# A graph-attention layer on one core: carried rows copied by ScalarE out of PSUM, h fetched for finished blocks, and a new order on the SP queue

## The chip, the cores and the metric

The kernel runs on one core of a Trainium2 chip. The metric is the device time of a run in microseconds (us), the median of several runs. Beside the runs there is one execution taken by the hardware profiler; the "profile" or "trace" below is that one.

An engine of the core works through its own instruction stream in order: TensorE (PE), VectorE (DVE), ScalarE (ACT), GpSimd (POOL) and SyncE (SP). SP computes nothing here: it issues nearly all plain DMAs. GpSimd issues the gathers.

## The reference

200,000 edges (src, dst), sorted by dst, join 12,500 nodes with 256 features; 8 heads of 32. What is computed, cut to what matters:

```python
h = jnp.maximum(_layernorm(x, axis=-1), 0.0)
q, k, v = h @ Wq + bq, h @ Wk + bk, h @ Wv + bv          # each (n, HEADS, D)
logits = einsum('ehd,ehd->eh', q[dst], k[src]) / sqrt(D)
expv   = exp(logits - segment_max(logits, dst)[dst])
attn   = expv / segment_sum(expv, dst)[dst]
agg    = segment_sum(attn[:, :, None] * v[src], dst)
y      = h + gelu(agg + h @ Wskip + bskip)
out    = x + (layernorm(y) * gamma + beta)
```

## The kernel before

**Front.** `project` walks over the nodes in 98 blocks of 128. For each it computes h (norm and Relu), and k and v by two matmuls, and stores h in the table `h_tab`, k|v (512 columns) in `kv_tab`, and the two factors of the norm (reciprocal root, shifted mean) in `st_tab`. Beside it `make_plan` reads the edges and works out the tables that the main loop walks by.

**The main loop.** `walk_streams` cuts the edges into 8 streams (S) and 66 steps (NST). In a step every stream goes over 384 slots, 3 tiles (K) of 128 partitions. Slot 0 is no edge: it holds what the stream has summed up so far for the node at which the step begins, the *carried row* (8 denominators and 256 sums). In the loop of a step c:

- `gather`: 24 indirect DMAs by GpSimd, one per tile and stream, fetch 128 rows of `kv_tab` into a tile `kv`. The pool has 5 such tiles, and a step uses 3. Tiles 0 and 1 of step c+1 are asked for at the beginning of step c, tile 2 after the first `weigh`.
- `windows` (two to three steps ahead): eight DMAs fetch the h of the nodes that each stream meets in a step, 32 or 64 rows per stream; `turn_windows` and `queries` make q of them on PE.
- `hot_e`, `hot_n`: 0/1 matrices from slots to nodes and back, made from `near`, `near_n` and `et`.
- `spread` (q to the slots, PE), `times` (q times k, DVE, L1058), `total` (sum per head, DVE, L1067), `turn` (transpose, PE).
- `maxima`: two scans and a subtraction (L1087 to L1090, DVE), then exp (L1091, ACT); `turn_back` (PE, L1098).
- `weights`: ACT copies the 64 denominators of the carried rows out of the kv tile's first partition (`wden`, L1105) and then the weights (`vw`, L1107). `weigh`: weight times v (DVE, L1114), and for tile 0 the weights times `wden` (L1119). A tile's `weigh` is the last use of its kv buffer.
- `add_up(c, i)`: the weighted rows are summed per node on PE, in three groups i of streams (0 to 3; 4 and 5; 6 and 7). ACT copies the sums from PSUM to SBUF (`sums_w`, L1142). `carry` (below) sends the last row of each stream's sums to partition 0 of the next step's first kv tile by DMAs, into columns 248 to 511: for i = 0 four DMAs (L1157), for i = 2 two (L1161) that serve four streams. Then the sums go to `table` (L1147).

A step's loop in the code begins with `times(c, 2)` and ends with `times(c+1, 1)` and `add_up(c, 2)`.

**Finished blocks.** When all sums of a pair of 128-node blocks are in `table`, the pair is finished beside the loop by class `Pair`, over three steps: `fetch` (sums, x and the norm's factors, six DMAs, L802 to L804), `norm` (h from x, two activations, L808), `turn`, `divisors`, `skip`, `divide`, `add`, `gelu`, `stats`, `root`, then `factors`, `normal`, `shifted`, `scale`, `store` (two DMAs, L891). There are 46 such pairs, and the six last ones (class `Last`) come after the loop, in the space of kv tiles.

**Order.** `keep` ties each instruction to the one before it on the same engine, so that the order of the code is the order on PE, DVE, ACT and SP. SP's order in a step with a pair, in `before`: six fetches, eight windows, two stores, four carries, four table writes, `et` and `pen` for step c+3, two table writes, two carries, two table writes. DMAs of a queue take turns at eight semaphores, so that a DMA is issued only when the eighth before it has landed.

Of the kernel before, what the change touches and what calls it, by code (L numbers as in the profile page):

```python
# [38 lines left out]
P = 128  # L39
# [5 lines left out]
S = 8  # L45
# [18 lines left out]
def gnn_kernel(ctx: ExitStack, tc: tile.TileContext, x, src, dst, Wq, bq, Wk, bk, Wv, bv,  # L64
# [17 lines left out]
    st_tab = dram.tile([NP, 2], F32, name="st_tab")  # L82
# [68 lines left out]
    def project():  # L151
# [12 lines left out]
        with tc.tile_pool(name="proj_c", bufs=1) as cpool, \  # L164
# [25 lines left out]
            def prepare(g):  # L190
# [14 lines left out]
                nr = pool.tile([P, 6, 2], F32, name="nr", bufs=3)[:, :n, :]  # L205
# [11 lines left out]
                return h, nr  # L217

            ready = {0: prepare(0)}
            for g, (b0, n) in enumerate(zip(starts, sizes)):  # L220
# [17 lines left out]
                h, nr = ready.pop(g)  # L238
# [9 lines left out]
                for tab, t in ((h_tab, h), (kv_tab, kvo), (st_tab, nr)):  # L248
                    nc.sync.dma_start(tab[b0 * P:(b0 + n) * P, :]
                                      .rearrange("(p b) d -> p b d", p=P), t)  # L250
# [21 lines left out]
    def finish(pool, psum, n, xt, sums, weights, mr, b_s, bet, o):  # L272
# [9 lines left out]
        h = pool.tile([P, n, HID], F32, name="h")  # L282
        for b in range(n):
            nc.scalar.activation(h[:, b, :], xt[:, b, :], AF.Relu, scale=mr[:, b, 1:2],
                                 bias=mr[:, b, 0:1])
# [46 lines left out]
    with tc.If(fits > 0) as branch:  # L332
        table = dram.tile([S, NT, SUMS], F32, name="table")
        walk_streams(tc, N, HID, NST, KL, ident, idx, d0_row, slot_row, near, near_n, e_tab, pen_tab,
                     h_tab, kv_tab, st_tab, table, x, out, w_q, w_s, one_row, b_q3, b_s3, b_o3,
                     gam, eps)
    with branch.Else():
# [4 lines left out]
        with tc.tile_pool(name="gfin", bufs=2) as pool, \  # L342
# [6 lines left out]
            for b0 in range(0, NBLK, NB):  # L349
                xt = pool.tile([P, NB, HID], F32, name="x_f")  # L350
                sums = pool.tile([P, NB, SUMS], F32, name="sums")
                mr = pool.tile([P, NB, 2], F32, name="mr_f")
# [9 lines left out]
                for t, tab, w in ((sums, gtab, SUMS), (mr, st_tab, 2)):  # L362
                    nc.sync.dma_start(t, tab[b0 * P:(b0 + NB) * P, :w]
                                      .rearrange("(b p) d -> p b d", p=P))
                s4 = sums.rearrange("p b (h d) -> p b h d", h=HEADS)
                finish(pool, psum, NB, xt, s4[:, :, :, :D], s4[:, :, :, D], mr, b_s, bet, o)
# [313 lines left out]
def make_near(tc, near, near_n, late):  # L680

    nc = tc.nc
    wide = S * WN
    with tc.tile_pool(name="near", bufs=1) as pool:
# [14 lines left out]
        for out, cols in ((near, wide), (near_n, near_n.shape[1])):  # L701
# [11 lines left out]
            else:  # L713
                for s, at in NARROW.items():
                    iota(grp[:, at:at + WNN], [[0, WNN]], s)
                iota(n[:, :P], [[0, 4], [1, WNN]])
                iota(n[:, P:], [[0, 4], [1, WN]])
# [18 lines left out]
            if cols < wide:  # L736
                ends = pool.tile([6 * S, 1], F32, name="near_e")
                nc.vector.tensor_sub(ends, pick[:, 3:4], pick[:, 5:6])
                for a, w in ((0, WNN), (P, WN)):
                    last = slice(a + w - 1, a + 4 * w, w)  # L740
                    nc.vector.tensor_scalar(out[:, last], grp[:, last], ends, None, op0=OP.mult)


def walk_streams(tc, N, HID, NST, KL, ident, idx, d0_row, slot_row, near, near_n, e_tab, pen_tab, h_tab,
                 kv_tab, st_tab, table, x, out, w_q, w_s, one_row, b_q3, b_s3, b_o3, gam,
                 eps):
# [31 lines left out]
    class Pair:  # L778
# [7 lines left out]
        def places(self):  # L786
            self.sums = self.pool.tile([P, 2, SUMS], F32, name="sums")
            self.x = self.pool.tile([P, 2, HID], F32, name="x_f")
            self.mr = self.pool.tile([P, 2, 2], F32, name="mr_f")
            self.h = self.pool.tile([P, 2, HID], F32, name="h", bufs=1)  # L790
# [6 lines left out]
        def fetch(self):  # L797
# [3 lines left out]
            for b, (node, row) in enumerate(zip(nodes, rows)):  # L801
                self.keep(nc.sync.dma_start(self.sums[:, b, :], tab[ds(row, P), :]))  # L802
                self.keep(nc.sync.dma_start(self.x[:, b, :], x[ds(node, P), :]))
                self.keep(nc.sync.dma_start(self.mr[:, b, :], st_tab[ds(node, P), :]))  # L804

        def norm(self):
            for b in range(2):
                self.keep(nc.scalar.activation(self.h[:, b, :], self.x[:, b, :], AF.Relu,  # L808
                                               scale=self.mr[:, b, 1:2], bias=self.mr[:, b, 0:1]))
# [79 lines left out]
        def store(self):  # L889
            for b, node in enumerate(loaded(slot_row[0:1, self.m, 0:2], N - P)):  # L890
                self.keep(nc.sync.dma_start(out[ds(node, P), :], self.y[:, b, :]))  # L891

    class Last(Pair):
# [3 lines left out]
        def __init__(self, pool, m, room, small, ps_h, ps_o, keep):  # L897
            Pair.__init__(self, pool, m, ps_h, ps_o, keep)
            self.room, self.mr = room, small
# [10 lines left out]
        def fetch_rows(self):  # L910
            self.places()
            for b, node in enumerate(loaded(slot_row[0:1, self.m, 0:2], N - P)):
                self.keep(nc.sync.dma_start(self.x[:, b, :], x[ds(node, P), :]))
                self.keep(nc.sync.dma_start(self.mr[:, b, :], st_tab[ds(node, P), :]))
# [6 lines left out]
    with ExitStack() as es:  # L921
# [199 lines left out]
        def add_up(c, i, tiles=range(K)):  # L1121
# [21 lines left out]
            if c + 1 < NST and i != 1:  # L1143
                carry(c, i)
            for s in streams:
                _, at, w = where(s)
                keep(nc.sync.dma_start(table[s, ds(g["nodes"][s], w - 1), :],  # L1147
                                       g["sums"][at:at + w - 1, i, :]))

        def carry(c, i):  # L1150


            sums, kv = step[c]["sums"], step[c + 1]["kv"][0][0:1, :, HID - HEADS:]
            if i == 0:
                for s, at in NARROW.items():
                    r = at + WNN - 1
                    keep(nc.sync.dma_start(kv[:, s:s + 1, :], sums[r:r + 1, 0:1, :]))  # L1157
            else:
                for b in range(2):
                    r = b * WN + WN - 1  # L1160
                    keep(nc.sync.dma_start(kv[:, 4 + b::2, :], sums[r:r + 1, 1:3, :]))  # L1161
# [28 lines left out]
        for j in range(K - 1):  # L1190
# [4 lines left out]
            turn(0, j)  # L1195
        pair = before = None
        for c in range(NST - 1):

            pair_next = None
            if c in due:  # L1200
# [5 lines left out]
                pair_next.fetch()  # L1206
# [7 lines left out]
            if pair:  # L1214
                pair.norm()
# [9 lines left out]
            if before:  # L1225
                before.scale()
                before.store()
# [15 lines left out]
            if tiles_of(c + 1) == K:  # L1243
                gather(c + 1, K - 1)
            if pair:
# [46 lines left out]
        assert len(rest) <= 6  # L1292
        mrs = one.tile([P, 6, 2, 2], F32, name="mr_l")
        lasts, banks = [], {}

        def room(i):
            if i % 2 == 0:
                room.tile = gath.tile([P, S, KV], F32, name="kv").rearrange("p s d -> p (s d)")
            half = S * KV // 2
            return room.tile[:, i % 2 * half:i % 2 * half + half]  # L1300

        def bank(i):
            def get():
                if i % 2 == 0:
                    banks[i // 2] = qe_ps.tile([P, 2, 2, HID], F32, name="ps_qe")
                return banks[i // 2][:, i % 2]
            return get

        def last(i):
            if i < len(rest):  # L1310
                lasts.append(Last(fin, rest[i], room(i), mrs[:, i],
                                  lambda: hot_ps.tile([P, 2, KC, P], F32, name="ps_hot"),
                                  bank(i), keep))
                lasts[i].fetch_rows()

        for i in range(6):
            last(i)
# [3 lines left out]
        if pair:  # L1321
            pair.norm()
        for j in range(tiles_of(c)):
# [3 lines left out]
            if tiles_of(c) == K and j == 1:  # L1327
                total(c, K - 1)
        if tiles_of(c) == K:
            turn(c, K - 1)  # L1330
        if before:
            before.shifted()
            before.scale()
            before.store()
        for p in lasts[:2]:
            p.norm()
# [17 lines left out]
        for p in lasts[2:4]:  # L1354
            p.norm()
# [5 lines left out]
        for i in range(3):  # L1361
            add_up(c, i, range(tiles_of(c) - 1, tiles_of(c)))
        for p in lasts:
# [9 lines left out]
        for p in lasts[2:4]:  # L1373
            p.turn()
            p.skip()
        for p in lasts[4:]:
            p.norm()
        if pair:
            pair.store()
        for i, p in enumerate(lasts):  # L1380
            if i > 3:
                p.turn()
                p.skip()
# [5 lines left out]
        for i in range(len(lasts) + 2):  # L1389
# [7 lines left out]
            if i > 1:  # L1397
                lasts[i - 2].scale()
                lasts[i - 2].store()
# [344 lines left out]
```

## Time and profile before

| | |
|---|---|
| median of 3 runs | 3814.16 us (3803.91 to 3824.61) |
| the profiled execution | 2578.42 us, its span 2576.5 us |
| busy, PE / DVE / ACT / POOL | 1901.7 / 1931.5 / 957.7 / 1602.2 us |
| DMA | 588.25 MB, mean 228 GB/s |
| mean granted TensorE clock | 0.859 |

The runs take 1236 us longer than the profiled execution; nothing in the profile shows what for. "Busy" is the time in which an instruction is shown on the engine. A line such as "L1015 POOL DMA_INDIRECT kv<-kv_tab,idx x1576 | ..., ... | ..." gives line, engine, operation, what it writes and reads and how often, then busy time in us, mean ns of one, idle time of the engine just before such instructions, and what ended most of it. In the lines of the waits, "A <- B: t, n, m" says that A's engine stood still before A for t us in n places, at most m, until B was done. A wait for several things is put down to the last of them.

### The profile page before, as it was taken

Reading aid. Unit: us, or ns where it says so; the run is one execution under the profiler, and the core shown is the slowest. Engines: PE = TensorE matmul, PEld = TensorE weight load, DVE = VectorE, ACT = ScalarE, POOL = GpSimd, SP = SyncE. Lnnn points to the kernel's source line nnn. Section 1 sums busy time; section 2 is a strip of 40 time slices with the busy share of each in tenths; the row PEclk is TensorE's granted clock in tenths of the full one; section 3 lists DMA queues with packets and bytes.
Section 4 is the critical chain, followed back from the end, with each engine's and each line's share of the span. In section 5 each row is a group of like instructions: output and inputs, shape, how many; then the busy total and the mean of one; then the engine's idle time right before and its main releaser. Section 6 shows DMA issues by size and latency. Waiting matters only on the chain.

```text
span 2576.5 us, 35985 instructions
## 1 busy us (share of the span) xinstructions
PE 1901.7 (74%) x10240; PEld 1092.2 (42%) x10240; DVE 1931.5 (75%) x2228; ACT 957.7 (37%) x2111; POOL 1602.2 (62%) x1646
## 2 busy tenths in 40 slices
PE   6898776767777677777777777776777777767765
PEld 3443443434444444444444444444444444444433
DVE  7886677777777777777777787777777787777774
ACT  3432222222443443343443343443443443443433
POOL 2301776667766667677666777666767767667730
PEclk9999778777888988888898888888988988888887
DMA  7966887777877777777777777777777878777742
GB/s 257 321 233 206 242 241 224 220 215 232 241 233 230 233 233 230 231 235 237 232 226 229 235 238 236 232 235 235 235 229 238 241 231 234 232 227 234 238 139 64
DMA packets 283677, 588.25 MB, mean 228 GB/s; under 512 B 69931, under 2 KB 173852, under 8 KB 281288
## 3 DMA queue, kind: packets, MB, share of 16 engines
q0 software_dynamic: 128736, 423.23, 55.4%
q1 hardware_dynamic: 154202, 162.16, 19.8%
q8 instruction: 83, 1.36, 0.2%
q14 instruction: 126, 1.03, 0.1%
q10 hardware_dynamic: 530, 0.47, 0.1%
HBM read 500.90 MB, written 84.21 MB: 227 GB/s over the span
## 4 chain that ended last, share of the span: by engine, by line
POOL 26%; DMA 24%; DVE 22%; issue 15%; PE 8%; SPq 3%; ACT 2%; DVEq 0%; ACTq 0%; POOLq 0%
POOL kv L1015 26%; DMA kv<-kv_tab,idx 12%; DVE vw L1114 8%; DMA table<-sums_w 6%; DVE prod L1058 5%; PE ps_kv L244 4%; DVE L L1067 4%; DMA kv<-sums_w 3%; DVE st L855 1%; DMA x_in<-in_x_dram 1%; PE ps_qe L1048 1%; DVE sums L851 1%; SPq L1157 1%; DMA hw<-h_tab 1%; DMA e_tab<-row 1%
## 5 line engine op out<-in xcount | busy, mean ns | idle before, releaser
L1015 POOL DMA_INDIRECT kv<-kv_tab,idx x1576 | 1558.6, 989 | 677.1 <-issue 418.5
L1114 DVE TENSOR_TENSOR vw<-ps_x,kv 128x2048 f32<-128x2048 f32 x197 | 444.6, 2284 | 478.0 <-ACT vw L1107 402.1
L1048 PE MATMUL ps_qe<-qw,to_e 64*128 64x256 f32 x3152 | 468.6, 426 | 117.5 <-DVE prod L1058 117.0
L1058 DVE TENSOR_TENSOR prod<-ps_qe,kv 128x1024 f32<-128x1024 f32 x394 | 463.7, 1218 | 19.0 <-DMA kv<-kv_tab,idx 8.4
L1067 DVE TENSOR_REDUCE L<-prod 128x64 f32<-128x2048 f32 x197 | 450.3, 2286 | 6.7
L1048 PEld LDWEIGHTS ps_qe<-qw,to_e 64*128 64x128 f32 x3152 | 302.3, 203 | 276.8 <-DVE prod L1058 226.8
L1008 PE MATMUL ps_hot<-w_q,hwT 128*128 128x256 f32 x792 | 323.8, 570 | 1.3 <-ACT hwT L994 1.1
L1025 PE MATMUL ps_hot<-et,near 48*128 48x384 bf16 x264 | 105.5, 400 | 276.5 <-ACT qw L1010 251.0
L1008 PEld LDWEIGHTS ps_hot<-w_q,hwT 128*128 128x128 f32 x792 | 211.5, 284 | 103.2 <-issue 57.4
L1133 PE MATMUL ps_a<-vw,to_n 128*32 128x264 f32 (+1 forms) x2356 | 240.0, 439 | 3.9 <-DVE vw L1119 2.9
L244 PE MATMUL ps_kv<-w_kv,hT 128*128 128x512 f32 x392 | 186.8, 620 | 23.8 <-ACT hT L137 22.9
L1142 ACT COPY sums_w<-ps_a 128x264 f32<-128x264 f32 x131 | 49.7, 379 | 393.5 <-PE ps_a L1133 389.5
L955 ACT ACT_TABLE_LOAD x138 | 177.1, 1283 | 2.4
L1010 ACT COPY qw<-ps_hot 128x256 f32<-128x256 f32 (+1 forms) x132 | 62.3, 472 | 237.0 <-PE ps_hot L1008 237.0
L1133 PEld LDWEIGHTS ps_a<-vw,to_n 128*32 128x32 f32 (+1 forms) x2356 | 92.2, 126 | 133.7 <-issue 70.9
L1027 ACT ACTIVATE to_e<-ps_hot,ones 128x384 f32<-128x384 f32 x264 | 143.4, 580 | 9.5 <-PE ps_hot L1025 6.1
L1105 ACT COPY wden<-kv 1x64 f32<-1x64 f32 x66 | 16.0, 242 | 343.3 <-DMA kv<-kv_tab,idx 177.9
L1038 ACT ACTIVATE to_n<-ps_hot,ones 128x384 f32<-128x384 f32 x197 | 107.2, 579 | 90.3 <-PE ps_hot L1036 88.9
L244 PEld LDWEIGHTS ps_kv<-w_kv,hT 128*128 128x128 f32 x392 | 72.0, 194 | 107.3 <-issue 71.3
L1004 PEld LDWEIGHTS <-one_row 3*128 3x128 bf16 x132 | 12.6, 95 | 239.2 <-issue 236.9
L839 PE MATMUL ps_a<-w_s,hT 128*128 128x256 f32 x368 | 93.5, 398 | 22.3 <-ACT hT L825 22.3
L994 ACT COPY hwT<-ps_hot 128x256 f32<-128x256 f32 (+1 forms) x132 | 61.7, 468 | 127.0 <-PE ps_hot L991 122.4
(280 smaller groups left out, 2109.8 us busy)
## 6 DMA issues: line engine op xcount, KB each, us to landing
kv<-kv_tab,idx POOLq DMA_INDIRECT x1576
kv_tab<-kvo SPq DMA_DIRECT2D x14, 1536.0 KB
table<-sums_w SPq DMA_DIRECT2D x264, 65.0 KB
hw<-h_tab SPq DMA_DIRECT2D x264, 64.0 KB
pen<-pen_tab SPq DMA_DIRECT2D x66, 192.5 KB
sums<-table SPq DMA_DIRECT2D x92, 132.0 KB
x_f<-in_x_dram SPq DMA_DIRECT2D x92, 128.0 KB
out_dram<-o SPq DMA_DIRECT2D x92, 128.0 KB
```

The source lines that it names most:

```text
L244: ins = nc.tensor.matmul(ps_kv, hT[:, c, :], w_kv[:, c, :], start=c == 0, stop=c == KC - 1)
L955: keep(nc.scalar.activation(dummy[:, 1:2], dummy[:, 0:1], function))
L1008: keep(nc.tensor.matmul(ps[:, b, :], g["hwT"][:, b, k, :], w_q[:, k, :], start=False, stop=k == KC - 1, skip_group_check=True))
L1015: nc.gpsimd.indirect_dma_start(out=t[:, s, :], out_offset=None, in_=kv_tab[:, :], in_offset=bass.IndirectOffsetOnAxis(ap=idx[:, s, j, c:c ...
L1025: keep(nc.tensor.matmul(ps[:, :CH], near[:, i * P:(i + 1) * P], step[c]["et"], start=True, stop=True))
L1027: keep(nc.scalar.activation(step[c]["to_e"][:, i, :], ps[:, :CH], AF.Relu, scale=-1.0, bias=ones))
L1038: keep(nc.scalar.activation(step[c]["to_n"][:, j, :], ps, AF.Relu, scale=-1.0, bias=ones))
L1048: keep(nc.tensor.matmul(ps[:, b, a, :], g["to_e"][r, 2 * half + a, j * P:(j + 1) * P], g["qw"][r, (half + a) * half, :], start=True, stop= ...
L1058: keep(nc.vector.tensor_tensor(g["prod"][:, four, :].rearrange("p (a b) d -> p a b d", a=2), g["qe", half].rearrange("p b a d -> p a b d") ...
L1067: keep(nc.vector.tensor_reduce(g["L"][:, j, :].rearrange("p (s h) -> p s h", s=S), g["prod"].rearrange("p s (h d) -> p s h d", h=HEADS), A ...
L1114: keep(nc.vector.tensor_tensor(t[:, :, HEADS:].rearrange("p s (h d) -> p s h d", h=HEADS), wj[:, :, :, None].to_broadcast([P, S, HEADS, D] ...
L1133: keep(nc.tensor.matmul(ps[at:at + w, :], g["to_n"][:, j, i * P + at:i * P + at + w], g["vw"][j][:, s, :], start=j == 0, stop=j == tiles_o ...
```

## The change

- Row order: each stream's window begins with the carried row. `near_n` is made with its numbers one lower, so that the first column (it was the last) stands for the node that goes on, and the table gets rows 1 to w-1 in place of 0 to w-2.
- The carry: right after the copy of the sums, ACT copies one row per stream from PSUM to partition 0 of the next kv tile. The six DMAs of a step and the function `carry` go.
- h of a finished pair comes from `h_tab` by a DMA; `norm`, the table `st_tab` and the fetch of the factors go. h has two buffers in place of one.
- SP's order: `pair_next.fetch()` comes after `store(0)` and the last gather of the step, then `store(1)`; the store of a pair is cut into its two DMAs.
- The tail: rows of the last pairs are fetched in step NST-2; the third to sixth of them are turned and multiplied (`turn`, `skip`) ahead of their sums, the fifth and sixth in PSUM banks of `xt_ps` and `ag_ps`.
- The fallback path (not taken here) fetches h too.

```diff
             keep(nc.scalar.copy(g["sums"][:, i, :], ps))
-            if c + 1 < NST and i != 1:
-                carry(c, i)
+            if c + 1 < NST:
+                for s in streams:
+                    at = where(s)[1]
+                    keep(nc.scalar.copy(step[c + 1]["kv"][0][0:1, s, HID - HEADS:],
+                                        ps[at:at + 1, :]))
             for s in streams:
                 _, at, w = where(s)
                 keep(nc.sync.dma_start(table[s, ds(g["nodes"][s], w - 1), :],
-                                       g["sums"][at:at + w - 1, i, :]))
-        def carry(c, i):
-            sums, kv = step[c]["sums"], step[c + 1]["kv"][0][0:1, :, HID - HEADS:]
-            if i == 0:
-                for s, at in NARROW.items():
-                    r = at + WNN - 1
-                    keep(nc.sync.dma_start(kv[:, s:s + 1, :], sums[r:r + 1, 0:1, :]))
-            else:
-                for b in range(2):
-                    r = b * WN + WN - 1
-                    keep(nc.sync.dma_start(kv[:, 4 + b::2, :], sums[r:r + 1, 1:3, :]))
+                                       g["sums"][at + 1:at + w, i, :]))
...
-                self.keep(nc.sync.dma_start(self.mr[:, b, :], st_tab[ds(node, P), :]))
-
-        def norm(self):
-            for b in range(2):
-                self.keep(nc.scalar.activation(self.h[:, b, :], self.x[:, b, :], AF.Relu,
-                                               scale=self.mr[:, b, 1:2], bias=self.mr[:, b, 0:1]))
+                self.keep(nc.sync.dma_start(self.h[:, b, :], h_tab[ds(node, P), :]))
...
-                pair_next.fetch()
             if c + 3 < NST:
                 windows(c + 3)
...
-            if pair:
-                pair.norm()
...
                 before.scale()
-                before.store()
+                before.store(0)
...
             if tiles_of(c + 1) == K:
                 gather(c + 1, K - 1)
+            if pair_next:
+                pair_next.fetch()
+            if before:
+                before.store(1)
+            if c == NST - 2:
+                for i in range(6):
+                    last(i)
...
-        for p in lasts[2:4]:
+        for p in lasts[2:]:
             p.turn()
             p.skip()
-        for p in lasts[4:]:
-            p.norm()
         if pair:
-            pair.store()
-        for i, p in enumerate(lasts):
-            if i > 3:
-                p.turn()
-                p.skip()
+            pair.store(0)
+            pair.store(1)
+        for p in lasts:
             p.divisors()
             p.divide()
```

## The prediction

> **What bounds the kernel now.** I read the page first, then the line view of the scan at L1087 (one per step), the waits of VectorE, GpSimd and the SP queue, and last the timeline of a few steps. The scan starts give the length of a step:
>
> ```profile
> L1087 DVE TENSOR_TENSOR_SCAN ps_x<-pen,ps_x x66: 635/902/962, 284.9 to 2495.4; 64x384 f32<-64x384 f32 x65, 64x256 f32<-64x256 f32 x1
> ```
>
> (2495.4 - 284.9) / 65 = 34.01 us per step; the steps take 2210 of the span's 2576.5 us. Who fills a step? These are rows of the page, the same waits over the whole run, and the SP queue's waits:
>
> ```profile
> L1015 POOL DMA_INDIRECT kv<-kv_tab,idx x1576 | 1558.6, 989 | 677.1 <-issue 418.5
> ...
> L1105 ACT COPY wden<-kv 1x64 f32<-1x64 f32 x66 | 16.0, 242 | 343.3 <-DMA kv<-kv_tab,idx 177.9
> ```
>
> ```profile
> POOL kv L1015 <- issue: 418.5, 1373, 0.3
> DVE vw L1114 <- ACT vw L1107: 402.1, 57, 11.7
> ...
> POOL kv L1015 <- DVE vw L1119: 106.7, 37, 5.5
> ```
>
> ```profile
> DVE vw L1114 <- DMA hw<-h_tab: 75.9, 9, 9.7
> DVE o L887 <- PE ps_hot L881: 28.3, 45, 3.4
> ```
>
> ```profile
> SPq L1147 <- DMA table<-sums_w: 255.8, 128, 3.7
> SPq L802 <- DMA table<-sums_w: 162.8, 48, 5.2
> SPq L891 <- DMA out_dram<-o: 135.1, 47, 4.3
> ```
>
> GpSimd issues 24 gathers a step at 0.989 + 0.305 us (418.5/1373): 24 x 1.294 = 31.1 us of 34.0. VectorE stands still at one place only, the first weigh of a step (L1114): 402.1 + 75.9 = 478 us, 7.2 us in each of 66 steps. It waits for ScalarE's copies at L1107, which stand behind the copy of the carried row at L1105, and that one is idle 343 us. The timeline of one step shows for what (start, duration, instruction; in brackets the idle time before):
>
> ```profile
> 1221.53 0.38 ACT L1142 COPY sums_w<-ps_a 128x264 f32<-128x264 f32 x1 [3.04 <-PE ps_a L1133]
> ...
> 1228.73 1.84 SPq L1161 DMA_DIRECT2D kv<-sums_w  x2
> ...
> 1229.35 0.52 ACT L1091 ACTIVATE W<-W 64x384 f32<-64x384 f32 x1
> ...
> 1238.83 0.24 ACT L1105 COPY wden<-kv 1x64 f32<-1x64 f32 x1 [7.44 <-DMA kv<-sums_w]
> ...
> 1239.31 2.29 DVE L1114 TENSOR_TENSOR vw<-ps_x,kv 128x2048 f32<-128x2048 f32 x1 [10.42 <-ACT vw L1107]
> ```
>
> The row to be carried is in SBUF at 1221.91. Its DMA stands 7 us in SP's queue and needs another 8.3 us (1230.57 to 1238.83) until ScalarE goes on; VectorE loses 10.42 us. Where that DMA was in time, near the end of the run, the same wait is:
>
> ```profile
> 2469.10 2.29 DVE L1114 TENSOR_TENSOR vw<-ps_x,kv 128x2048 f32<-128x2048 f32 x1 [1.85 <-ACT vw L1107]
> ```
>
> The POOL row above closes the circle: the weigh frees the kv buffer for the next gathers, so GpSimd idles too (106.7 us booked on L1119, more on DMAs that released it later). So the carry sets the step, with GpSimd's own 31.1 us close beneath.
>
> [...]
>
> **The change part by part.**
>
> *Carry.* Six DMAs a step go (390 in all: x260 and x130). With them goes the wait at L1105 for a landing. What is late next: exp (0.52), in steps with a finished block the table load and its dummy (1.28 + 0.20), the wden copy (0.24) and two weight copies (0.30). That is the 1.85 us above; VectorE's part of such a step, from 1272.83 to the end of the divide at 1300.75, is 27.92 us without the wait. 27.92 + 1.85 = 29.8 us, below GpSimd's 31.1. Steps without a block are shorter on VectorE by the stats, factors, scale, divisors and divide (1.7 + 0.4 + 2.0 + 0.4 + 0.7 = 5.2 us) and fall on GpSimd more clearly.
>
> *Eight copies on ScalarE.* 1x264 from PSUM. The nearest rows: L1105 (1x64) 0.242, L1142 (128x264, same source and length) 0.379 us. I take 0.379: 3.0 us a step; the low end is 1.9. Behind the four of the first group stand the copy at L1078 and the next sums copy, behind the last two the normal() of the older block. In the step at 1250 the four would end about 1253.4, the root about 1254.7 against its need on VectorE at 1256.93; the last two would end at 1258.6, normal at 1259.7, needed at 1261.92. norm() leaves just this place (two activations, 1.09 us for the pair at 1221.81). So I charge nothing; if the cover were gone, 3.0 - 1.1 = 1.9 us a step, 124 us.
>
> *h fetched.* 46 pairs and 6 last ones, two blocks each, 128 KB in place of 1 KB: 104 x 128 KB = 13.6 MB on top of 588.25 (2.3%). Rows and h are asked for after store(0), in the step shown about 1264 to 1268, and turned in the next one at about 1295, 27 us later; the wait for the table writes (162.8 us on SP) falls away since those landed long before. Charge 0; the high end, if bytes set the time, comes as a rival.
>
> *SP's order.* 32 DMAs a step become 26; the fetch no longer stands ahead of the eight windows, and the second store no longer waits for the first with all the rest behind it. Nothing on SP feeds the recurrence of a step any more: windows are needed two steps later, table writes one step later (sums_w has one buffer, its next write is a step away). Charge 0.
>
> *Front.* st_tab's small stores go (14 of 6 KB and a few smaller), SP has slack there: 0 to -3 us; I take 0.
>
> *Tail.* The turn of the last full pair waited 6.17 us on PE for its hT, because ScalarE stood at norm() of rows just fetched; those norms and late rows go: -6. The turns of the fifth and sixth pair lie between 2536 and 2544, after the sums came; moved ahead, they lie beside the 8.7 us of sums DMAs: I take -5 (bounds 0 and -8). Together -11.
>
> *Sum.* A step goes to GpSimd's 31.1; I add 0.3 for coupling, since a gather may start only some 2.4 us after the weigh and VectorE at 29.8 leaves 1.3 us of room: 31.4. (34.01 - 31.4) x 65 = 170. With the tail -181: span 2576.5 to 2395.
>
> **From the profile to the time.** The profiled execution took 2578.42 us, the runs' median is 3814.16: 1236 us more, of which no view shows anything (the span leaves 1.9 us around it). Either it is a constant beside the kernel, and then 3814 - 181 = 3633; or it stretches all, 3814 x 2397/2578 = 3546; or the gathers are slower there, (3814 - 366) / 66 = 52 us a step, and then the carry's wait may lie in their shadow. Nothing in the profile decides; I take the constant, the plainest, and let the others widen the range.
>
> **The rivals.**
> 1. *Part of the stall comes back.* VectorE and GpSimd meet at one buffer, ScalarE's copies cost 1.9 us where I charged nothing: step 32.7, 85 + 11 = 96 less: 3718. For: no cover on ScalarE is over 3 us. Against: every such wait is absent in the step at 2469.
> 2. *The gap stretches with the kernel:* 3546.
> 3. *Nothing to gain in the runs:* gathers at 52 us a step hide the carry; only the tail shows: 3803. For: the unexplained 1236 us. Against: no engine is slow in the profile.
> 4. *Slower: bytes set the time.* Place: the DMA engines, queue q1 beside q0. The runs move 588.25 MB in 3814 us, 154 GB/s; 13.6 MB of h at that rate is 88 us, less 11 in the tail: 3891. It decides where the bytes of a step take longer than GpSimd's 31.1 us. For: busy share 0.79 in mid-run. Against: slice two of the page moved 321 GB/s, and a step at 31.4 us needs about 8.15 MB / 31.4 = 260.
> 5. *The carry still waits* (ScalarE's write to a row that a gather or VectorE still holds): the tile was gathered and its products taken before that copy, so I give it no number of its own; it falls under 1.
>
> **Chances.** Forecast 0.44, rival 1 0.17, rival 2 0.13, rival 3 0.08, rival 4 0.18. Within 0.5% (19 us, about what a measurement can tell from no change) lies rival 3 alone. Faster 0.74, same 0.08, slower 0.18. The range for 8 in 10 runs from 3510 (rival 2 with the 0.3 us of coupling gone: 19 us, and the tail's bound) to 3830, which leaves rival 4 out.
>
> **What would show it.** Right: L1157 and L1161 have no successor; VectorE's wait at the weigh is about 2 us; the scan's mean distance is 31 to 31.8 us; POOL's idle time besides issue falls from 259 (677.1 - 418.5) to under 100 us; ScalarE's busy time rises by some 197 - 52 = 145 us. Wrong: a new wait at L1058 for kv (gathers too late), POOL's issue gap growing beyond 0.305, landings that stretch, or a mean over 33. If the profile falls to about 2395 and the median does not move by as much, the step from profile to run was the wrong one.

## The result, and the profile after

| | before | changed |
|---|---|---|
| median of 4 runs | 3813.19 us (3803.91 to 3824.61) | 3776.2 us (3760.45 to 3781.26) |
| ratio | | 0.9895 [0.9853, 0.9936] |
| profiled execution | 2578.42 us, span 2576.5 | 3781.26 us, span 3779.5 |
| busy PE / DVE / ACT / POOL | 1901.7 / 1931.5 / 957.7 / 1602.2 us | 2353.9 / 1940.7 / 1080.3 / 1563.4 us |

Faster, by 1.05%, which is little but clear of the scatter (the runs of the two kernels do not overlap), and not by the 4.8% of the forecast. The two profiles cannot be set beside each other: that of the changed kernel is as long as its timed runs, that of before was 1236 us shorter than its own. So the profile after shows what the profile before did not, namely where the long runs spend their time. First the scan that marks the steps (view of one tile: duration min/median/max in ns, first and last start in us), then a row of the page and the waits:

```profile
L1078 DVE TENSOR_TENSOR_SCAN ps_x<-pen,ps_x x66: 635/902/962, 332.7 to 3705.4; 64x384 f32<-64x384 f32 x65, 64x256 f32<-64x256 f32 x1
```

```profile
L1006 POOL DMA_INDIRECT kv<-kv_tab,idx x1576 | 1523.1, 966 | 1893.8 <-DVE vw L1110 1397.4 <-issue 457.1 <-DMA kv<-kv_tab,idx 16.8
```

```profile
ACT sums_w L1133 <- remote: 1531.3, 96, 28.6
POOL kv L1006 <- DVE vw L1110: 1397.4, 63, 36.1
DVE rstd L855 <- ACT rstd L851: 759.0, 45, 21.8
...
PE ps_a L1124 <- issue: 410.1, 231, 6.2
...
DVE vw L1105 <- ACT vw L1098: 156.5, 66, 4.4
```

A step takes (3705.4 - 332.7) / 65 = 51.89 us. The last row is the wait that the change was about: 156.5 / 66 = 2.4 us a step, so the carry no longer holds VectorE up. The gathers are no slower than in the first profile (966 ns beside 989, and 457.1 / 1418 = 0.32 us of issue between them). What is new is the first row: ScalarE, which copies the sums of `add_up` out of PSUM, stands still 1531 us, 23 us a step, for something the view calls remote, that is, it found no instruction that ended just then. The semaphore that came last is TensorE's in all 96 of these waits; where a copy also waits for DMAs, these had landed at least 28 us before. GpSimd and VectorE stand behind it. The timeline shows one such wait (start, duration, instruction; idle time before in brackets):

```profile
1517.45 2.27 PE L1039 MATMUL ps_qe<-qw,to_e 64*128 64x256 f32 x16 [0.86 <-DVE prod L1049]
...
1519.65 0.66 PE L1124 MATMUL ps_a<-vw,to_n 128*32 128x264 f32 x8
...
1521.13 1.56 PE L1124 MATMUL ps_hot<-vw,to_n 128*64 128x264 f32 x12
...
1528.44 1.23 DVE L1049 TENSOR_TENSOR prod<-ps_qe,kv 128x1024 f32<-128x1024 f32 x1 [4.49 <-remote]
...
1534.03 0.28 PEld L1039 LDWEIGHTS ps_qe<-qw,to_e 64*128 64x128 f32 x1 [1.81 <-issue]
...
1537.55 0.38 ACT L1133 COPY sums_w<-ps_a 128x264 f32<-128x264 f32 x1 [19.87 <-remote]
```

The eight matmuls at 1519.65 are the last that the copy at 1537.55 needs, so their result is there only some 17 us after the trace shows them. This is the rule in such a trace: from the recorded end of these matmuls to the first copy of a step's sums it is 13.1 us here (median of 66 steps). I read this as matmuls that TensorE finishes well after their recorded end; that is my reading of these times, and no view shows what TensorE does in between. The windows of the same stretch (us; PE busy and count, PEld, DVE, ACT, POOL, granted clock, DMA share, GB/s):

```profile
1515.00:1520.00 5.00, 3.97 (x42) 1.95 (x40) 4.96 (x4) 2.66 (x5) 3.78 (x5) 1.00 0.72 206
1520.00:1525.00 5.00, 2.91 (x27) 1.48 (x20) 3.64 (x7) 0.00 (x0) 3.87 (x4) 1.00 0.61 190
1525.00:1530.00 5.00, 1.12 (x6) 0.55 (x7) 1.52 (x2) 0.00 (x0) 3.81 (x4) 0.86 0.71 202
1530.00:1535.00 5.00, 3.18 (x8) 1.46 (x8) 1.99 (x1) 0.00 (x0) 3.82 (x4) 0.50 0.72 208
1535.00:1540.00 5.00, 0.57 (x3) 0.29 (x3) 0.00 (x0) 1.75 (x5) 3.81 (x4) 0.50 0.70 203
```

42 matmuls appear in the first 5 us, then 27, 6, 8 and 3, while GpSimd goes on issuing gathers (3.8 of each 5 us). When the matmuls dry up at 1525 the recorded clock is still 1.00; it falls to 0.50 at 1528.6 (the record moves in steps of about 3.4 us). VectorE's product at 1528.44 waits for the second eight of the row at 1517.45, which ends at 1519.72: TensorE was nearly 9 us late before the record fell. From there to the copy at 1537.55 only the eight matmuls at 1519.65 are left in the order of the code, and they take 9 us where the record shows 0.66. So a clock halved at 1528.6 does not account for this wait. What the clock has to do with it in the whole run is counted further down.

### The profile page after: what moved, and what is told of

It reads as the page before. It is cut to its first block, busy times and chain, and to the rows that moved or that the text cites. A ratio compares the mean times of both kernels' runs of the same rounds, so it can differ in the third digit from the quotient of the medians.

```text
span 3779.5 us, 34981 instructions
## 1 busy us (share of the span) xinstructions
PE 2353.9 (62%) x10240; PEld 1275.8 (34%) x10240; DVE 1940.7 (51%) x2228; ACT 1080.3 (29%) x2527; POOL 1563.4 (41%) x1646
## 3 DMA queue, kind: packets, MB, share of 16 engines
q0 software_dynamic: 128736, 423.23, 38.3%
## 4 chain that ended last, share of the span: by engine, by line
another core or an unknown queue 42%; PE 31%; ACT 12%; DVE 7%; issue 6%; DMA 1%; DVEq 0%; ACTq 0%; SPq 0%; POOL 0%; POOLq 0%
PE ps_qe L1039 7%; PE ps_hot L999 5%; PE ps_kv L243 4%; ACT kv L1139 3%; PE ps_a L829 3%; DVE prod L1049 2%; PE ps_hot L871 2%; PE ps_a L1124 2%; ACT L946 2%; ACT to_e L1018 1%; ACT hwT L985 1%; DVE vw L1105 1%; PE ps_a L834 1%; PE ps_hot L982 1%
## 5 line engine op out<-in xcount | busy, mean ns | idle before, releaser
L1006 POOL DMA_INDIRECT kv<-kv_tab,idx x1576 | 1523.1, 966 | 1893.8 <-DVE vw L1110 1397.4
L1039 PE MATMUL ps_qe<-qw,to_e 64*128 64x256 f32 x3152 | 757.5, 540 | 562.1 <-issue 389.2
L1039 PEld LDWEIGHTS ps_qe<-qw,to_e 64*128 64x128 f32 x3152 | 458.0, 258 | 821.0 <-issue 555.1
L1124 PE MATMUL ps_a<-vw,to_n 128*32 128x264 f32 (+1 forms) x2356 | 396.0, 479 | 474.1 <-issue 410.1
L1105 DVE TENSOR_TENSOR vw<-ps_x,kv 128x2048 f32<-128x2048 f32 x197 | 444.7, 2285 | 156.5 <-ACT vw L1098 156.5
L1058 DVE TENSOR_REDUCE L<-prod 128x64 f32<-128x2048 f32 x197 | 450.4, 2286 | 6.7
L1124 PEld LDWEIGHTS ps_a<-vw,to_n 128*32 128x32 f32 (+1 forms) x2356 | 131.3, 140 | 738.3 <-issue 642.8
L999 PE MATMUL ps_hot<-w_q,hwT 128*128 128x256 f32 x792 | 249.3, 460 | 35.6 <-ACT hwT L985 35.3
L999 PEld LDWEIGHTS ps_hot<-w_q,hwT 128*128 128x128 f32 x792 | 164.8, 223 | 124.4 <-issue 60.5
L946 ACT ACT_TABLE_LOAD x138 | 177.1, 1283 | 2.4
L1124 PE MATMUL ps_hot<-vw,to_n 128*64 128x264 f32 x796 | 131.5, 400 | 49.2 <-issue 47.2
L1133 ACT COPY sums_w<-ps_hot 128x264 f32<-128x264 f32 x67 | 25.4, 379 | 435.0 <-remote 420.7
L1139 ACT COPY kv<-ps_a 1x264 f32<-1x264 f32 x390 | 143.9, 369 | 6.3
```

Of the source, the lines that this page charges most:

```text
L946: keep(nc.scalar.activation(dummy[:, 1:2], dummy[:, 0:1], function))
L999: keep(nc.tensor.matmul(ps[:, b, :], g["hwT"][:, b, k, :], w_q[:, k, :], start=False, stop=k == KC - 1, skip_group_check=True))
L1006: nc.gpsimd.indirect_dma_start(out=t[:, s, :], out_offset=None, in_=kv_tab[:, :], in_offset=bass.IndirectOffsetOnAxis(ap=idx[:, s, j, c:c ...
L1039: keep(nc.tensor.matmul(ps[:, b, a, :], g["to_e"][r, 2 * half + a, j * P:(j + 1) * P], g["qw"][r, (half + a) * half, :], start=True, stop= ...
L1058: keep(nc.vector.tensor_reduce(g["L"][:, j, :].rearrange("p (s h) -> p s h", s=S), g["prod"].rearrange("p s (h d) -> p s h d", h=HEADS), A ...
L1105: keep(nc.vector.tensor_tensor(t[:, :, HEADS:].rearrange("p s (h d) -> p s h d", h=HEADS), wj[:, :, :, None].to_broadcast([P, S, HEADS, D] ...
```

## The experiments

The runs came to five different chips, each time with the kernel before beside them. The chip (or the condition it was in; no chip was seen in both) turned out to matter more than any edit. In the column of before, 2588.41 and 2588.02 are medians of seven executions, and 2406.96 is one of four; the others in the table are single executions, as are all times below for which no range is given:

| chip | before | changed kernel | with plain transfers | gathers, fixed index |
|---|---|---|---|---|
| 4 | 2588.41 us | | 2228.76 | |
| 15 | 2588.02; 2596.47 | 2406.96 | | 2378.7 |
| 3 | 2576.1 | | | 2374.72 |
| 1 | 3822.28; 3830.12 | | 2242.48 | |
| 10 | 3816.9 | | | 3757.4 |

The median of the result belongs with chips 1 and 10 (before 3813), the profile before with chips 3, 4 and 15. Chips 4, 15 and 3 are called short below, 1 and 10 long. Letters of theories are explained where an expectation brings them in.

**On chip 4: the kernel before again, one part alone, one part undone, and the gathers replaced.**

`e0_before` is the kernel before without an edit:

> The kernel before, unchanged, to get a profile of a run that takes as long as the runs of the median. Theory A (the runs are held up by TensorE: while gathers land, its matmuls are finished many times later than their length, and everything that waits for them stands still): time 3.80 to 3.83 ms, a step of about 53 us, ScalarE's copies of the sums and VectorE's products wait for TensorE for over 10 us a step, and VectorE's wait at the first weigh (7.2 us a step in the 2578 us execution) is not what sets the step. Theory B (the same picture as in the 2578 us execution, only that each gather costs GpSimd more): 3.80 to 3.83 ms too, but a gather takes 2 us of GpSimd instead of 0.989 us and GpSimd has no idle time but issue. If the time is about 2580 us again, both are open and the chip differs from that of the runs.

2593.39 us, step (2509.5 - 284.0) / 65 = 34.24 us, and VectorE's wait for the carry as in the first profile:

```profile
DVE vw L1114 <- ACT vw L1107: 419.6, 57, 13.1
...
DVE vw L1114 <- DMA hw<-h_tab: 70.6, 9, 9.4
```

So the same kernel needs 2.59 ms here and 3.81 ms elsewhere; 1236 us that every run pays beside the kernel are ruled out.

`e1_carry_act` is the kernel before with the carry alone changed (and the row order that it needs); h is computed by `norm` as before, SP's order is the old one but for the six DMAs that go:

```diff
...
-            if c + 1 < NST and i != 1:
-                carry(c, i)
+            if c + 1 < NST:
+                for s in streams:
+                    at = where(s)[1]
+                    keep(nc.scalar.copy(step[c + 1]["kv"][0][0:1, s, HID - HEADS:],
+                                        ps[at:at + 1, :]))
...
```

> The kernel before with one part of the change: the carried row first in its window and copied by ScalarE out of PSUM; h is still computed, SP's order is the old one less the six carries. Theory A: the carry lies in the shadow of TensorE's wait, ratio to before 0.990 to 1.000, in any case not below 0.985. Theory C (the carry was on the path in the runs too, and the rest of the change lost what it won): ratio 0.95 or lower.

2396.69 us (2392.42 to 2406.74), ratio 0.9264 [0.9222, 0.9306]; step (2315.5 - 284.8) / 65 = 31.24 us.

```profile
POOL kv L1015 <- issue: 438.1, 1438, 0.3
...
DVE vw L1114 <- ACT vw L1107: 159.6, 66, 5.6
```

The carry alone brings all that the change brings on such a chip.

`e2_carry_dma` is the changed kernel with the carry sent by DMAs again:

```diff
-            if c + 1 < NST:
...
-                    keep(nc.scalar.copy(step[c + 1]["kv"][0][0:1, s, HID - HEADS:],
-                                        ps[at:at + 1, :]))
+            if c + 1 < NST and i != 1:
+                kv = step[c + 1]["kv"][0][0:1, :, HID - HEADS:]
+                if i == 0:
+                    for s, r in NARROW.items():
+                        keep(nc.sync.dma_start(kv[:, s:s + 1, :], g["sums"][r:r + 1, 0:1, :]))
...
```

> The changed kernel with the carry sent by DMAs again (from the first row of the window), all else as in the change: h fetched, SP's new order, the new tail. Theory A: ratio to before 0.990 to 1.000. Theory C: above 1.02, since then h and the new order cost what the carry wins.

2507.16 us (2505.22 to 2513.22), ratio 0.9688 [0.965, 0.9727]; step (2422.6 - 284.4) / 65 = 32.90 us.

```profile
DVE vw L1105 <- ACT vw L1098: 287.1, 47, 10.6
DVE vw L1105 <- DMA hw<-h_tab: 117.7, 19, 10.3
```

The rest of the change, without the new carry, shortens the step by 34.24 - 32.90 = 1.34 us. It touches the same wait from the other end: a carry goes out earlier. From the end of a step's last copy of sums to the end of the issue of its last carry it is 6.71 us in e0 and 5.34 here (mean of 65 steps), and the two rows of VectorE's wait add up to 490 us there and 405 here, 1.3 us a step less. That SP's new order does this, and not the fetch of h, is likely but was not tried by itself. The two gains overlap: once the row goes by ScalarE the rest is worth nothing (e1 on chip 4 against the changed kernel on chip 15, 31.24 and 31.43 us).

`e3_plain_pool` is the changed kernel with a plain transfer in place of each gather; the rows that the index names are left out, 256 KB of fixed contiguous rows are fetched:

```diff
-                nc.gpsimd.indirect_dma_start(
-                    out=t[:, s, :], out_offset=None, in_=kv_tab[:, :],
-                    in_offset=bass.IndirectOffsetOnAxis(ap=idx[:, s, j, c:c + 1], axis=0))
+                nc.gpsimd.dma_start(t[:, s, :], kv_tab[(s * 3 + j) * P:(s * 3 + j + 1) * P, :])
```

> The changed kernel with each indirect gather replaced by a plain DMA from GpSimd of the same 256 KB out of fixed, contiguous rows of the k|v table (the gather by index is left out, so the output is another one). Bytes, destinations, the queue and the buffers stay. Theory A1 (TensorE is held up by data landing in SBUF at some 200 GB/s): time stays within 5% of 3776 us. Theory A2 (it is held up by what is special in an indirect gather[...]): time falls below 2900 us.

2228.76 us; step (2152.7 - 278.6) / 65 = 28.83 us. With GpSimd relieved the next bound is 2.6 us below the 31.43 of the changed kernel (`e4_after`, next), near what the prediction gave VectorE (29.8 us in a step with a finished block, 5.2 less in one without). On this chip the run could not tell what holds TensorE up elsewhere, since it was not held up to begin with.

**On chip 15: the changed kernel itself, and h computed again.**

> The changed kernel, unchanged, beside the kernel before on one chip. Theory D (what differs between the 2578 us of the first profile and the 3776 us of the result is the chip or its condition, not the kernel): where the kernel before takes 2.58 to 2.60 ms, this one takes 2.36 to 2.41 ms, ratio 0.915 to 0.93, as the carry alone gave 0.926; where the kernel before takes 3.8 ms, this one takes 3.76 to 3.78 ms, ratio 0.985 to 0.995. Theory E (the changed kernel itself holds TensorE up while gathers land): 3.76 to 3.78 ms even where the kernel before takes 2.59 ms.

`e4_after`, the changed kernel without an edit: 2406.96 us (2402.7 to 2409.76), ratio 0.9298 [0.9257, 0.9338]. Its scan, GpSimd's row, its waits, and two windows of the stretch shown above (same columns):

```profile
L1078 DVE TENSOR_TENSOR_SCAN ps_x<-pen,ps_x x66: 634/902/962, 284.0 to 2326.7; 64x384 f32<-64x384 f32 x65, 64x256 f32<-64x256 f32 x1
```

```profile
L1006 POOL DMA_INDIRECT kv<-kv_tab,idx x1576 | 1546.2, 981 | 522.1 <-issue 434.3
```

```profile
POOL kv L1006 <- issue: 434.3, 1410, 4.8
ACT sums_w L1133 <- PE ps_a L1124: 345.7, 130, 11.0
...
DVE vw L1105 <- ACT vw L1098: 160.6, 66, 5.5
...
DVE prod L1049 <- DMA kv<-kv_tab,idx: 103.9, 41, 7.9
```

```profile
1520.00:1525.00 5.00, 3.96 (x35) 1.78 (x31) 4.91 (x8) 2.20 (x8) 3.78 (x5) 1.00 0.89 308
1525.00:1530.00 5.00, 3.98 (x29) 2.26 (x29) 4.89 (x6) 2.87 (x7) 3.78 (x5) 1.00 0.78 229
```

A step is (2326.7 - 284.0) / 65 = 31.43 us. Besides its own issuing GpSimd stands still 522.1 - 434.3 = 88 us, where it was 259 in the first profile: it waits for hardly anybody, which is how an engine looks that sets the time. ScalarE waits for the sums 345.7 us where it was 1531, and TensorE takes 35 and 29 matmuls per 5 us beside the same gathers. Theory D holds here, E falls.

`e5_no_hfetch` is the changed kernel with h computed from x and the factors again (`st_tab`, `norm` and the fetch of the factors put back):

```diff
-                self.keep(nc.sync.dma_start(self.h[:, b, :], h_tab[ds(node, P), :]))
+                self.keep(nc.sync.dma_start(self.mr[:, b, :], st_tab[ds(node, P), :]))
...
+        def norm(self):
+            for b in range(2):
+                self.keep(nc.scalar.activation(self.h[:, b, :], self.x[:, b, :], AF.Relu,
+                                               scale=self.mr[:, b, 1:2], bias=self.mr[:, b, 0:1]))
```

> The changed kernel with h of the finished blocks computed from x by two activations as before (factors of the norm fetched), all else as in the change: ScalarE's carry, SP's new order, the new tail. Difference to the changed kernel: 13.6 MB of DMAs against 104 activations. Theory D on a chip with 2.59 ms: within 0.7% of the changed kernel, since both are covered. If the h bytes cost time: at least 1% faster than the changed kernel. If ScalarE has no room for norm beside the carry's copies: 1% slower or more.

2407.95 us (2400.77 to 2412.59), ratio 0.9289 [0.9244, 0.9333]: no difference to the changed kernel. On such a chip the 13.6 MB cost nothing and save nothing.

> The kernel before once more, for its profile on the same chip as the two above. On a chip with 3.8 ms, theory A: TensorE finishes late while gathers land, ScalarE's copies of the sums wait for it over 10 us a step, gathers still take about 0.99 us of GpSimd each. On a chip with 2.59 ms: the profile of e0_before again, within 1%.

`e6_before_again`, the kernel before, on this chip: 2593.55 us, as on chip 4.

**On chip 1 (before 3822.28 us): before with a profile, and the plain transfers.**

> The kernel before, unchanged, for a profile on a chip of the kind on which it takes 3.8 ms, if this call comes to one. Theory D1 (there TensorE ends its matmuls late while gathers land, in the kernel before as in the changed one): the step of its loop is about 52 us, ScalarE waits some 20 to 29 us for add_up's matmuls in most steps, the gathers are still about 1 us of GpSimd each, and the wait of DVE vw for ACT vw is under 3 us a step, since it lies in the shadow of TensorE. Theory D2 (the kernel before is long there for another reason, its gathers or its small transfers): gathers well over 1.3 us each or the wait of DVE vw above 10 us a step. On a chip where it takes about 2590 us this says nothing new: span about 2590 and a step of 34 us.

`e7_before_slow`, the kernel before without an edit: 3830.12 us, and this is the execution that was profiled: a profile as long as the runs of the result.

```profile
L1087 DVE TENSOR_TENSOR_SCAN ps_x<-pen,ps_x x66: 635/902/962, 332.2 to 3747.7; 64x384 f32<-64x384 f32 x65, 64x256 f32<-64x256 f32 x1
```

```profile
ACT sums_w L1142 <- remote: 1564.3, 59, 30.3
DVE prod L1058 <- remote: 953.0, 88, 25.5
...
POOL kv L1015 <- DVE vw L1119: 799.4, 35, 34.6
...
DVE vw L1114 <- ACT vw L1107: 186.2, 61, 7.7
```

Step (3747.7 - 332.2) / 65 = 52.55 us, gathers 967 ns each, ScalarE 1564 us behind TensorE: theory D1. The first copy of a step's sums comes 25.9 us after the recorded end of its matmuls (median); in e0 and in e4 it is 0.07 us, at most 0.13. The wait that the change removes is here 186.2 us in all, 2.8 us a step, where it was 419.6 on chip 4. D2 falls.

> The changed kernel with a plain transfer of the same 256 KB in place of each gather by index (the rows that the index names are not fetched). On a chip where the kernel before takes 3.8 ms: theory A1 (any data landing in SBUF at this rate holds TensorE up): above 3300 us, with ScalarE still waiting over 15 us for add_up's matmuls. Theory A2 (only the gathers by index do[...]): under 2500 us. On a chip where before takes 2590 us: 2230 us, as the same kernel took before, which tells the two not apart.

`e8_plain_slow`, the kernel of `e3_plain_pool` on this chip: 2242.48 us, step (2167.9 - 286.3) / 65 = 28.95 us.

```profile
L1006 POOL DMA_DIRECT2D kv<-kv_tab x1576 | 854.9, 546 | 1041.2 <-DVE vw L1108 651.5
```

```profile
POOL kv L1006 <- DVE vw L1108: 651.5, 63, 13.1
ACT sums_w L1131 <- PE ps_a L1122: 330.8, 127, 10.9
```

On the chip where before takes 3822 us, the kernel with plain transfers is 14 us from its time on chip 4 (2228.76), and ScalarE waits 330.8 us for the sums in place of 1564, with the first copy again 0.07 us behind its matmuls. It lands the same bytes, at 267 GB/s over the span where the gathers there moved 153. So data landing does not hold TensorE up (A1 falls), the gathers by index do (A2). By what way these make TensorE late on the same chip (25.9 us in e7), no run shows.

**On chips 15, 3 and 10: the addresses or the instruction.** `e9_fixed_index`, `e11_fixed_index` and `e13_fixed_index` are one kernel: the gather instruction is kept, but all its indices are overwritten so that they name the same contiguous rows as the plain transfers (the rows of the plan are not fetched):

```diff
+        nc.gpsimd.iota(idx, pattern=[[K * P, S], [P, K], [0, NST]], base=0, channel_multiplier=1)
         walk_streams(tc, N, HID, NST, KL, ident, idx, d0_row, slot_row, near, near_n, e_tab, pen_tab,
```

`e10_half_plain` and `e12_half_plain` have plain transfers for the even streams alone:

```diff
             for s in range(S):
+                if s % 2 == 0:
+                    nc.gpsimd.dma_start(t[:, s, :], kv_tab[(s * 3 + j) * P:(s * 3 + j + 1) * P, :])
+                    continue
                 nc.gpsimd.indirect_dma_start(
```

> The changed kernel, still gathering by index, but every index names the same contiguous rows that the plain transfers read (the rows that the plan asks for are not fetched). GpSimd about 0.97 us a gather as before. On a chip where the kernel before takes 3.8 ms: theory A2a (the scattered addresses hold TensorE up) 2230 to 2450 us, ScalarE's wait for add_up under 5 us a step; theory A2b (the gather instruction itself does, wherever its rows lie) 3600 us or more, with that wait above 15 us a step. On a chip where before takes 2590 us it tells them not apart: about 2400, since GpSimd's issuing is what bounds it there.

> The changed kernel with every second gather (the even streams) made a plain transfer of the same size; the rows of those streams are not the ones that the plan asks for. On a chip where before takes 3.8 ms: if each gather by index holds TensorE up by its share, half of the 1370 us between the changed kernel and the one with plain transfers is left, about 2900 to 3000 us; if a few gathers at a time do no harm[...], 2300 to 2450; if any do the full harm, 3600 or more. On a chip where before takes 2590 us: between 2230 and 2407, near 2300, and nothing told.

Chip 15: 2378.7 and 2248.06 us.

```profile
L1007 POOL DMA_INDIRECT kv<-kv_tab,idx x1576 | 1526.9, 969 | 508.6 <-issue 435.6
```

Neither tells anything of the question, as the expectations say; the first shows that GpSimd's issuing, not the scatter of the rows, sets the 31 us step (969 ns a gather with contiguous rows).

> The kernel of e9_fixed_index again (gathers by index, all naming the same contiguous rows; the rows of the plan are not fetched). On a chip where before takes 3.8 ms: theory A2a (scattered addresses hold TensorE up) 2230 to 2450 us; theory A2b (the gather instruction does) 3600 us or more. On a chip where before takes 2590 us: 2379 us, as the same kernel took before, nothing told.

> The kernel of e10_half_plain again (every second gather a plain transfer of fixed rows). On a chip where before takes 3.8 ms: harm by the number of gathers, about 2900 to 3000 us; no harm from few at a time, 2240 to 2450; full harm from any, 3600 or more. On a chip where before takes 2590 us: 2248 us, as the same kernel took before, nothing told.

Chip 3: 2374.72 and 2234.05 us; the same again.

> The kernel of e9_fixed_index again (gathers by index, all naming the same contiguous rows; the rows of the plan are not fetched). On a chip where before takes 3.8 ms: theory A2a (scattered addresses hold TensorE up) 2230 to 2450 us; theory A2b (the gather instruction does) 3600 us or more. On a chip where before takes 2590 us: 2379 us, nothing told.

Chip 10, before 3816.9 us: 3757.4 us, step (3681.4 - 329.2) / 65 = 51.57 us.

```profile
ACT sums_w L1134 <- remote: 1531.6, 55, 28.9
POOL kv L1007 <- DVE vw L1111: 1402.1, 63, 32.9
```

With contiguous rows TensorE is held up as before (A2a falls, A2b stands): the first copy comes 25.6 us behind its matmuls. The plain transfers of e8 go over the same queue with as many packets and bytes (128736, 423.23 MB) from the same rows to the same places. So it is the gather instruction, wherever its rows lie; what of it, GpSimd's longer work for each (947 ns here, 546 in e8) or something else in it, is not separated. How the harm goes with the number of gathers was not seen, because no run of the half-plain kernel came to such a chip.

The last question is what the clock has to do with it. Counted from the traces: matmuls recorded as starting, per us of the stretches in which GpSimd issues its gathers or transfers without a gap of 0.6 us or more (from 400 us on to 200 us before the end); in all, then apart by the granted clock on record at the time, which is either 1.00 or 0.50; and the share of these stretches at 0.50:

```
                                all   clock 1.00   clock 0.50   share at 0.50
before, chip 4                 4.57      5.01         3.18           24%
before, chip 1                 2.32      4.36         1.01           61%
changed, chip 15               4.65      5.18         2.74           22%
changed, chip of the result    2.70      4.83         1.08           57%
plain transfers, chip 1        5.72      6.07         3.17           12%
fixed index, chip 10           2.51      4.60         0.91           57%
```

On a long chip matmuls start at about half the rate while gathers are issued, and most of the loss lies where the record says 0.50. Such times are longer there, and they are emptier: about one matmul per us, where a short chip at the same 0.50 starts about three. The three long traces have 66 stretches at 0.50 of 20 us or more each, about one a step; no other trace has more than eight. So half a clock by itself is not the explanation, but the clock is no bystander either. Which of the two brings the other about, the late matmuls or the 0.50, no run separates.

A step of the long kind then adds what otherwise overlaps. Its 24 gathers take 24 x (0.966 + 0.32) = 31 us, in which TensorE starts half its matmuls. GpSimd then waits 1397.4 / 66 = 21 us until TensorE, and VectorE behind it, have caught up and freed the buffers. 31 + 21 = 52 us, against 51.9 measured.

## Why the prediction was right and wrong

- **The step, 34.01 to 31.4 us: right, on the kind of chip where the profile before was taken.** Measured 34.24 (e0) to 31.43 (e4), and VectorE's wait at the weigh is 160.6 / 66 = 2.4 us (named: about 2). GpSimd is the bound by the signs that were named: idle time besides issue 522.1 - 434.3 = 88 us (named: under 100), and a step of 28.83 us once its instruction is cheaper (e3).
- **Eight copies at nothing: right.** 369 ns each against the 379 taken; ScalarE's busy time rose from 957.7 to 1076.9 us, 119 and not 145, and e1 with the copies in place has the shortest step of the chip-4 kernels that gather all rows.
- **h at nothing: right** (e5). **SP's order at nothing: right beside the new carry;** that without it the rest of the change saves 1.34 us a step (e2), most likely by this order, was not seen, since it was not asked what the order does to the old carry.
- **The tail, -11 us: too large.** From the last scan to the end 2591.2 - 2509.5 = 81.7 us (e0; 80.0 in e6) became 2400.8 - 2326.7 = 74.1: -6 to -8.
- **The sum, -181 us: right there:** 2588.02 to 2406.96 is -181.1 on chip 15. That it meets the forecast to the microsecond is luck: the two profiles of that chip (e6, e4) are 2591.4 - 2400.8 = 190.6 us apart, with more in the steps than the 170 of the forecast and less in the tail. Rival 1 (ScalarE's copies give part of the saving back) and rival 4 (bytes) fall with it; the slices in the middle of e4 moved 242 to 272 GB/s.
- **A sign was badly chosen.** "A new wait at L1058 for kv" was to show the forecast wrong. It came (103.9 us in e4, 12.2 in e0), with the step as forecast: a VectorE that waits for GpSimd's gathers is what one would expect when GpSimd is the bound.
- **From the profile to the time: this step failed.** "I take the constant, the plainest" turned 3814 - 181 into 3633. The 1236 us are no constant. They lie inside the steps, 52.55 - 34.24 = 18.3 us in each, 1190 us over 65 steps, and the rest in the front (the first scan is at 332 us in place of 284). In such a step the carry's wait lies in TensorE's shadow: 186.2 us at the weigh in e7 and 156.5 in the changed kernel, 0.45 us a step. The step itself is shorter by 52.55 - 51.89 = 0.66 us, 43 us in all, and the tail by 6.5 (80.6 to 74.1); these come from one profile each, and not of the same chip. The span of e7 and that of the changed kernel differ by 48.8 us, the medians of the result by 37.
- **Rival 3 was nearest to the outcome** (52 us a step, the carry hidden, 3803 us for the 3776 measured) but named the wrong engine: the gathers are issued as fast as ever, TensorE is late. It was given 0.08 because "no engine is slow in the profile". That was no argument: a profile that is 1236 us shorter than the runs, with 1.9 us around its span, had not seen what the runs do. Rival 2 (the gap stretches with the kernel) falls too: the ratio is 0.9895 on the one kind of chip and 0.9298 on the other.

Open is why TensorE is late under the gather instruction on some chips and not on others, and what part the clock has in it. Shown are the instruction (A2b), the engine, and that it does not need scattered rows. What the two share was not found, and apart from the fixed index no edit that keeps the gathers was run on such a chip.

## What to carry to other kernels

When the profiled execution and the timed runs differ by much more than the span leaves around it (here 1236 us against 1.9), the profile is of another condition: a saving read from it holds for that condition alone, and a second profile as long as the runs comes before any forecast. A wait is worth removing only where nothing slower covers it: the same edit brought 7% on one chip and 1% on another, because a later engine had become the bound. Where two parts of a change work on one wait, each alone shows a gain, and the gains do not add (here ratios of 0.9264 and 0.9688 alone, 0.9298 for the whole).

## What the runs showed of the hardware

- The same kernel took 2576 to 2601 us on chips 3, 4 and 15, and 3817 to 3830 us on chips 1 and 10 (three executions in all on these two).
- On the latter, while GpSimd issues gathers by index, matmuls start at half the rate (2.32 per us against 4.57), and the first copy of a step's sums comes 25.9 us after the recorded end of its matmuls (before on chip 1; 13.1 us for the changed kernel in the result, 0.07 us on chips 4 and 15); VectorE's, ScalarE's and GpSimd's instructions keep their durations (scan 902 ns, copy 378 against 379 ns, gather 967 against 990 ns). It goes with the instruction, not with the bytes: 2242 us with plain transfers on chip 1.
- Each of the three profiles of the long kind has 66 stretches of 20 us or more at a granted clock of 0.50, about one a step; in the gathers matmuls then start at 0.9 to 1.1 per us, against 2.7 to 3.2 at the same 0.50 on chips 4 and 15.
- A 256 KB transfer of contiguous rows costs GpSimd 546 to 548 ns as a plain one (e8, e3) and 947 to 969 ns as a gather by index (e13, e9).
- A table load of ScalarE took 1283 ns (mean of 138, the same in the profile before, e0, e4 and e7).
- In the profile before, SP's DMAs go round eight semaphores (2051 of 2078 carry that of the eighth DMA ahead of them). Of the 239 times that one of them stood waiting for another DMA to land, 150 were for that eighth one.
